# A four-layer attention and FFN kernel: the masked keys of the 16-head attentions made by VectorE, the norm's epsilon added there, a group's norm issued behind the keys ahead of it, and the mask loaded earlier

## The chip, the cores and the metric

The kernel runs on one core of a Trainium2 chip. Its time is the device time of one launch in microseconds, and the number that is compared is the median over several launches. A core has five engines with an instruction stream each: TensorE (PE in the profile; PEld is its weight load), VectorE (DVE), ScalarE (ACT), GpSimd (POOL) and SyncE (SP). An engine runs its stream in order and waits for the others by semaphores.

## The reference

`x` and `ctx_1024` are 16 blocks of 128 rows by 128 features, `mask` marks keys. Eight residual steps follow, each on the layer-normed x. This change is about the attentions of layers 0, 1 and 3:

```python
x = x + _L0_xattn_ref(_layernorm(x), ctx_1024, mask, wq, bq, wk, bk, wv, bv, wo, bo)
x = x + _L0_ffn_ref(_layernorm(x), ...)
x = x + _L1_xattn_ref(_layernorm(x), ctx_1024, ctx_1024, ...)
x = x + _L1_ffn_ref(_layernorm(x), ...)
x = x + _L2_xattn_ref(_layernorm(x), ctx_1024, ...)
x = x + _L2_ffn_ref(_layernorm(x), ...)
x = x + _L3_xattn_ref(_layernorm(x), ctx_1024, ctx_1024, ...)
x = x + _L3_ffn_ref(_layernorm(x), ...)

# layer 0's attention: 16 heads of 8 features, queries from x, keys and values from the context
attn = jnp.einsum('bhsd,bhtd->bhst', q, k) / math.sqrt(HD)
m = mask[:, None, None, :].astype(attn.dtype)
attn = attn * m - 100000.0 * (1.0 - m)
attn = jax.nn.softmax(attn, axis=-1)
o = jnp.einsum('bhst,bhtd->bhsd', attn, v)
return o.transpose(0, 2, 1, 3).reshape(b, s, NH * HD) @ wo + bo
```

Layer 1's attention scales each row of scores by a temperature that a small network reads from the scores' statistics; layer 3's is causal. The norm is `(x - m) / sqrt(v + 1e-5)`.

## The kernel before

X lies in SBUF throughout, as 16 blocks of 128 x 128 in 4 groups (NG = 4) of 4 blocks (GB = 4). Seven phases follow one another: attention of layer 0, its FFN, attention of layer 1, FFN of layer 1 together with the attention of layer 2, FFN of layer 2 (a product-key lookup), attention of layer 3, its FFN. `heads_attention` (L286) is called for layers 0, 1 and 3.

**Scores of 16 heads at once.** A head has 8 features. The 32 partitions of a row group hold 4 heads; so that one matmul with 32 rows gives the scores of 4 heads side by side, the keys K (128 x 512 of a group) are written four times into Kb, each time multiplied by a column of `c.gmask`, which keeps every fourth head and makes the rest zero (L341, L342). `s` = Q times Kb (in `negated_maxima`) gives a block's scores in two PSUM tiles of two banks, VectorE takes the negated maxima of each (L410, `nm`), GpSimd splits them into bfloat16 parts (`split`, L424 to L430), TensorE transposes them (`turn`), and the scores are computed once more, transposed and shifted (`st`), for the exponentials pT (L482, L552, L554). `av` is the sum over keys of V and of ones, `inv` (L474) the reciprocal, oT the normalized result, `po` the output projection that is added to X. In layer 1 (`warm`) GpSimd also squares the exponentials (L484).

**The order.** The loop at the end of `heads_attention` goes over steps i, in each of which different blocks are at different stages: maxima are `ahead` steps ahead of the exponentials (5, in layer 1 11). A new group's stages come with its first blocks: `begin_norm(n)`, then a step later `begin_turn(n)`, then `begin_queries(n)`. The matmuls of s, st and av are chained by `mmo`, so TensorE keeps their order; the rest of each engine's stream is put in order by the scheduler of the framework, over the whole program and by its own priorities.

**begin_norm** (L321 to L343): `layernorm` takes bn_stats and bn_aggr on VectorE (L239, L240), the reciprocal root by `rsqrt` on GpSimd, an addition of epsilon (`ve`, L231) and a power (`rstd`, L232), and then four tensor_scalars on VectorE for xn (L249, one buffer). GpSimd adds the output bias to X (L325). TensorE makes pk, VectorE (layer 0, with bias and mask, L333) or ScalarE (L337, L339) makes K of it, and GpSimd the four parts of Kb (one buffer, so that the next group's Kb waits for the last s of this one). `rsqrt` is used by all norms of the program (44 times), `begin_norm` by the three attentions with 4 groups each.

**The start.** On ScalarE's DMA queue stand the four loads of X and then the mask, broadcast to 128 partitions (L216); `mk`, a small second view of the mask, follows in layer 0's attention (L619). `pen` (L614) and `keys_out` (L621) are made of them by VectorE. The V buffers are cleared by GpSimd (L310), in space that the context's load leaves free when TensorE has transposed it.

**PSUM.** One pool of 2 one-bank buffers ("m": pt, pk, pq, pv, pm, av, po) and one of 3 two-bank buffers ("s": s and st).

Of the kernel before, what the change touches and what calls it, by code (L numbers as in the profile page):

```python
# [2 lines left out]

# [1 line left out]

# [7 lines left out]
U8 = mybir.dt.uint8  # L13
# [6 lines left out]
P = 128  # L20
NB = 16
# [159 lines left out]
def build(ctx: ExitStack, tc: tile.TileContext, x, ctxt, mask, packs, cols, out):  # L181
    nc = tc.nc
    PS = bass.MemoryType.PSUM
    const = ctx.enter_context(tc.tile_pool(name="const", bufs=1))
# [6 lines left out]
    X = const.tile([P, NB, P], F32, name="X")  # L191
    sb = {}
    widest = max(packs[name].shape[1] for name in packs)

    def load(name):

        n = packs[name].shape[1]
        if name == "c":
            t = const.tile([P, n], F32, name="consts")
        else:  # L200
            t = weights.tile([P, widest], F32, name="weights")
        nc.sync.dma_start(t[:, :n], packs[name])
        for key, (n, c, w) in cols[name].items():
            sb[f"{name}.{key}"] = t[:n, c : c + w]

    load("c")
    for n in range(NG):
        gb = slice(n * GB, (n + 1) * GB)
        nc.scalar.dma_start(X[:, gb, :], x.rearrange("b s d -> s b d")[:, gb, :])
    ident = sb["c.ident"]  # L210
    identb = const.tile([P, P], BF16, name="identb")
    nc.vector.tensor_copy(identb, ident)
    minus_half = const.tile([P, GB], F32, name="minus_half")
    nc.gpsimd.memset(minus_half, -0.5)
    mask_sb = const.tile([P, NB * P], U8, name="mask_sb")
    nc.scalar.dma_start(mask_sb, mask.rearrange("b s -> (b s)").partition_broadcast(P))  # L216

    def ps1(name):
        return psm.tile([P, 512], F32, tag="m", name=name)
# [4 lines left out]
    def mm(o, lhsT, rhs, start=True, stop=True):  # L224
        return nc.tensor.matmul(o, lhsT=lhsT, rhs=rhs, start=start, stop=stop)  # L225

    def rsqrt(o, v, eps):

        w = v.shape[-1]
        ve = small.tile([P, w], F32, tag="rs_v")  # L230
        nc.gpsimd.tensor_scalar_add(ve, v, eps)  # L231
        nc.gpsimd.tensor_tensor(o, ve, minus_half[:, :w], ALU.pow)  # L232

    def moments(xin, eps=1e-5):

        st = small.tile([P, GB, 6], F32, tag="ln_st")
        mv = small.tile([P, GB, 2], F32, tag="ln_mv")
        for b in range(GB):
            nc.vector.bn_stats(st[:, b, :], xin[:, b, :])  # L239
            nc.vector.bn_aggr(mv[:, b, :], st[:, b, :])  # L240
        rstd = small.tile([P, GB], F32, tag="ln_rstd")
        rsqrt(rstd, mv[:, :, 1], eps)
        return mv, rstd

    def layernorm(o, xin):

        mv, rstd = moments(xin)
        for b in range(GB):
            nc.vector.tensor_scalar(  # L249
                o[:, b, :], xin[:, b, :], mv[:, b, 0:1], rstd[:, b : b + 1], ALU.subtract, ALU.mult  # L250
            )
# [16 lines left out]
    def grp(n):  # L268
        return slice(n * GB, (n + 1) * GB), slice(n * GT, (n + 1) * GT)
# [16 lines left out]
    def heads_attention(pk, scale, keep=None, cmask=None, cmaskT=None, warm=False):  # L286
# [15 lines left out]
        with tc.tile_pool(name=f"at_{pk}", bufs=2) as wk:  # L302
# [5 lines left out]
            for j in range(2):  # L308
                v = wk.tile([P, GB, 4, 160], F32, name=f"V{j}", bufs=1)
                nc.gpsimd.memset(v.rearrange("p b r x -> p (b r x)"), 0.0)  # L310
                Vs.append(v)
            group = {}
# [8 lines left out]
            def begin_norm(n):  # L321
                gb, _ = grp(n)
                xn = wk.tile([P, GB, P], F32, name="xn", bufs=1)
                layernorm(xn, X[:, gb, :])
                nc.gpsimd.tensor_add(  # L325
                    X[:, gb, :], X[:, gb, :], w["bo"].unsqueeze(1).to_broadcast([P, GB, P])
                )
                group[n] = {"xn": xn, "nm": wk.tile([P, GB, 16], F32, name="nm", bufs=alive)}
                pk = ps1("pk")
                mm(pk, w["wk"], ctxT[:, grp(n)[1]])  # L330
                K = wk.tile([P, GT], F32, name="K", bufs=alive)
                if keep is not None:
                    nc.vector.scalar_tensor_tensor(  # L333
                        K, pk, w["kb"], mask_sb[:, grp(n)[1]], ALU.add, ALU.mult
                    )
                elif "kb" in w:
                    nc.scalar.activation(K, pk, AF.Identity, bias=w["kb"])  # L337
                else:
                    nc.scalar.copy(K, pk)  # L339
                Kb = wk.tile([P, 4, GT], F32, name="Kb", bufs=1)  # L340
                for g in range(4):  # L341
                    nc.gpsimd.tensor_scalar_mul(Kb[:, g, :], K, sb["c.gmask"][:, g : g + 1])  # L342
                group[n].update({"K": K, "Kb": Kb})  # L343

            def begin_turn(n):
                xT = wk.tile([P, GT], F32, name="xT", bufs=1)
# [238 lines left out]
            for i in range(-ahead - 3, NB + 2):  # L585
                pTs = exponents(i) if 0 <= i < NB else None
                if late is not None:
                    weighted(i - 1, late)
                late = pTs
                if due(i - 1 - GB) is not None:  # L590
                    finish(due(i - 1 - GB))
                if warm:
                    if squares is not None:
                        measured(i + before - 1, *squares)
                    squares = squared(i + before) if 0 <= i + before < NB else None
                if 0 <= i + ahead < NB:
                    negated_maxima(i + ahead)

                if due(i + ahead - GB) is not None:
                    turn(due(i + ahead - GB))  # L600
                if warm and due(i + 1) is not None:
                    turn(due(i + 1))
                if due(i + 2) is not None:
                    begin_values(due(i + 2))
                for k, stage in enumerate((begin_queries, begin_turn, begin_norm)):
                    if due(i + ahead + 1 + k) is not None:
                        stage(due(i + ahead + 1 + k))
# [631 lines left out]
    def layer2_ffn():  # L1239
# [6 lines left out]
        with tc.tile_pool(name="f2w", bufs=2) as wk:  # L1246
# [13 lines left out]
            def begin(n):  # L1260
                gb, _ = grp(n)
                xn = wk.tile([P, GB, P], F32, name="xn", bufs=1)
                layernorm(xn, X[:, gb, :])
                sq = wk.tile([P, GB, P], F32, name="sq", bufs=1)
                ms = small.tile([P, GB], F32, tag="ms")
                nc.vector.tensor_mul(sq, xn, xn)
                nc.vector.tensor_reduce(ms, sq, AX.X, ALU.add)
                nc.vector.tensor_scalar_mul(ms, ms, 1.0 / P)
                inv = small.tile([P, GB], F32, tag="inv")
                rsqrt(inv, ms, 1e-6)  # L1270
                nc.vector.tensor_mul(xn, xn, inv.unsqueeze(2).to_broadcast([P, GB, P]))
                xT = wk.tile([P, GT], F32, name="xT")
                transposed(xT, xn, lambda o, i: nc.vector.tensor_scalar_mul(o, i, w["norm_w"]))
                G = wk.tile([P, 8, GT], F32, name="G")
                for c in range(8):
                    pg = ps1("pg")
                    mm(pg, w["down"][:, c * P : (c + 1) * P], xT)
                    nc.scalar.activation(G[:, c, :], pg, AF.Gelu)
                group[n] = xT, G
# [203 lines left out]
```

## Time and profile before

| | us |
|---|---|
| median of 3 runs | 1607.78 (1598.61 to 1611.15) |
| the profiled execution | 1602.65 |
| its span, first to last instruction | 1600.8 |
| busy: TensorE, its weight loads | 1249.8, 880.1 |
| busy: VectorE, GpSimd, ScalarE | 957.3, 589.2, 525.4 |
| mean granted TensorE clock | 0.856 of full |
| layer 0's attention, first score matmul | 35.55 |
| layer 1's attention, first score matmul | 555.45 |
| layer 3's attention, first score matmul | 1430.10 |

The span and the busy times are of the one profiled execution; the median is of other launches, and lies 5.1 us above that execution. The profile's page gives the span in 40 slices of 40 us each. Busy shares in tenths, the granted TensorE clock in tenths, and the DMA's:

```profile
PE   4788799898989677887777756557778787878996
DVE  4566364565455665644634465557789887875552
ACT  1343455554544335554223421212001010014431
POOL 5532000000000366552222032148878878844310
PEclk7798799999999778989668977669798998889996
```

Layer 0's attention lies in the first four to five slices, layer 1's from slice 14 on (GpSimd at 3 to 6 by the squares), layer 2's lookup in slices 28 to 36 (GpSimd mostly at 7 or 8), layer 3's attention in 36 to 39. In layer 0's FFN (slices 5 to 13) GpSimd is nearly idle. An entry of the list of waits names who waited for whom, the total, how often and the longest; an entry of the timeline gives the start, the length, the engine, the line, the operation and tiles, and in brackets the idle time before and who ended it.

### The profile page before, as it was taken

The numbers are of one execution on the slowest core, as the hardware profiler recorded it, in microseconds if no ns is written. First come the engines' busy times: TensorE is split into PE (matmuls) and PEld (weight loads), VectorE is DVE, ScalarE is ACT, GpSimd is POOL, SyncE is SP. The second block draws the span as 40 slices with busy tenths as digits, with TensorE's granted clock in tenths as the row PEclk, the third lists the DMA queues.
The fourth block names the chain that finished last, engine by engine and source line by source line (L and its number), as shares of the span: only waits on it lengthen the run. The fifth ranks groups of instructions, "written<-read, shape, count | busy, mean of one in ns | idle before, by whom it ended". The sixth has DMA issues, their size and how long they took to land. (4 is left out here: it accounts for less than half of the span.)

```text
span 1600.8 us, 24944 instructions
## 1 busy us (share of the span) xinstructions
PE 1249.8 (78%) x10088; PEld 880.1 (55%) x10088; DVE 957.3 (60%) x2404; ACT 525.4 (33%) x836; POOL 589.2 (37%) x656
## 2 busy tenths in 40 slices
PE   4788799898989677887777756557778787878996
PEld 2355477676768434555555634434666666644556
DVE  4566364565455665644634465557789887875552
ACT  1343455554544335554223421212001010014431
POOL 5532000000000366552222032148878878844310
PEclk7798799999999778989668977669798998889996
DMA  4000000000000200000322020000000000000000
GB/s 150 1 2 17 0 0 1 1 0 1 1 1 1 99 1 1 2 2 2 106 68 78 24 87 1 1 9 1 1 1 1 1 1 1 1 6 1 2 2 27
DMA packets 26002, 28.05 MB, mean 18 GB/s; under 512 B 3360, under 2 KB 23712, under 8 KB 25376
## 3 DMA queue, kind: packets, MB, share of 16 engines
q1 hardware_dynamic: 20544, 23.06, 4.4%
q0 software_dynamic: 1024, 2.10, 0.4%
q10 hardware_dynamic: 4320, 1.31, 0.4%
q8 instruction: 79, 1.29, 0.3%
q14 instruction: 35, 0.29, 0.1%
HBM read 18.86 MB, written 7.60 MB: 17 GB/s over the span
## 5 line engine op out<-in xcount | busy, mean ns | idle before, releaser
L1328 POOL TENSOR_TENSOR C<-sim 128x1024 f32<-128x1024 f32 x128 | 241.5, 1919 | 48.9 <-PE psim L225 26.2
L231 POOL TENSOR_SCALAR ve<-mv 128x4 f32<-128x4 f32 x44 | 10.5, 240 | 543.6 <-DVE mv L240 516.2
L1349 PE MATMUL pc<-consts,C 128*128 128x128 f32 x1024 | 147.2, 297 | 51.3 <-POOL C L1328 26.6
L1349 PEld LDWEIGHTS pc<-consts,C 128*128 128x128 f32 x1024 | 127.2, 154 | 74.8 <-issue 38.8
L225 PE MATMUL pc<-hm,weights 128*128 128x256 f32 x640 | 155.1, 380 | 0.7 <-DVE hm L757 0.7
L1347 DVE MATCH_REPLACE8 C<-m,C 128x1024 f32<-128x1024 f32 x128 | 153.6, 1203 | 0.0
L410 DVE TENSOR_REDUCE nm<-s 128x8 f32<-128x1024 f32 x96 | 113.2, 1217 | 56.9 <-PE s L225 56.4
L225 PEld LDWEIGHTS pc<-hm,weights 128*128 128x128 f32 x640 | 120.9, 190 | 19.4 <-DVE hm L757 3.3
L474 DVE RECIPROCAL inv<-av 128x128 f32<-128x128 f32 x48 | 46.0, 957 | 109.1 <-PE av L225 109.0
L225 PE MATMUL s<-Kb,Q 32*128 32x512 f32 x384 | 76.9, 739 | 30.1 <-POOL Kb L342 25.4
L554 ACT ACTIVATE pT<-st 128x1024 f32<-128x1024 f32 x64 | 62.2, 1020 | 59.1 <-PE st L225 59.1
L225 PE MATMUL st<-Qb,K 32*128 32x512 f32 x512 | 79.4, 628 | 0.0
L342 POOL TENSOR_SCALAR Kb<-K,consts 128x512 f32<-128x512 f32 x48 | 74.4, 1567 | 9.1 <-PE s L225 9.0
L484 POOL TENSOR_TENSOR E<-pT 128x1024 f32<-128x1024 f32 x32 | 60.0, 1893 | 47.9 <-ACT pT L482 47.9
L757 DVE TENSOR_TENSOR hm<-he,M 128x512 f32<-128x512 f32 x64 | 40.7, 686 | 38.7 <-ACT he L753 38.7
L225 PEld LDWEIGHTS av<-pT,V 128*32 128x32 f32 x1536 | 42.2, 115 | 37.6 <-issue 25.8
L249 DVE TENSOR_SCALAR xn<-X,mv,rstd 128x128 f32<-128x128 f32 x112 | 51.8, 581 | 9.9 <-PE pt L257 8.2
L424 POOL CAST nms<-nm 128x16 bf16<-128x16 f32 x64 | 14.7, 255 | 116.3 <-DVE nm L410 92.6
L225 PE MATMUL av<-pT,V 128*32 128x128 f32 x1536 | 56.4, 288 | 0.6 <-DVE V L383 0.4
L225 PEld LDWEIGHTS s<-Kb,Q 32*128 32x128 f32 x384 | 23.0, 209 | 54.8 <-POOL Kb L342 30.3
L225 PE MATMUL av<-pT,consts 128*32 128x128 f32 x1536 | 52.2, 276 | 0.0
L1288 ACT COPY sim<-psim 128x512 f32<-128x512 f32 x16 | 9.4, 585 | 128.4 <-PE psim L225 128.4
(345 smaller groups left out, 2757.1 us busy)
## 6 DMA issues: line engine op xcount, KB each, us to landing
weights<-in_f SPq DMA_DIRECT2D x1, 3852.5 KB, 11.7
weights<-in_f SPq DMA_DIRECT2D x1, 2863.5 KB, 14.0
weights<-in_f SPq DMA_DIRECT2D x1, 2816.5 KB, 9.3
rows<-zero SPq DMA_DIRECT2D x2, 1344.0 KB, 11.5
rows_sb<-rows SPq DMA_DIRECT2D x14, 192.0 KB, 3.9
outs<-y SPq DMA_DIRECT2D x14, 192.0 KB, 2.0
weights<-in_a SPq DMA_DIRECT2D x1, 1088.5 KB
X<-in_x ACTq DMA_DIRECT2D x4, 256.0 KB, 5.0
```

The source lines that it names most:

```text
L225: return nc.tensor.matmul(o, lhsT=lhsT, rhs=rhs, start=start, stop=stop)
L249: nc.vector.tensor_scalar(o[:, b, :], xin[:, b, :], mv[:, b, 0:1], rstd[:, b : b + 1], ALU.subtract, ALU.mult)
L342: nc.gpsimd.tensor_scalar_mul(Kb[:, g, :], K, sb["c.gmask"][:, g : g + 1])
L410: nc.vector.tensor_reduce(nm[:, b, 8 * u : 8 * u + 8], ss[u].rearrange("p r (g k) -> p (r g) k", g=4), AX.X, ALU.max, negate=True,)
L424: nc.gpsimd.tensor_copy(at[:, b, :, :, 0], of[:, b])
L474: nc.vector.reciprocal(y, s)
L484: nc.gpsimd.tensor_mul(E2, E, E)
L554: nc.scalar.activation(pT, st, AF.Exp)
L757: nc.vector.tensor_mul(hm[:, k, c : c + 2, :], he, M[:, k, c : c + 2, :])
L1328: nc.gpsimd.tensor_add(C, sim[:, h, 0, :].unsqueeze(2).to_broadcast(sh), sim[:, h, 1, :].unsqueeze(1).to_broadcast(sh),)
L1347: nc.vector.match_replace(at, m8[:, h, :], at, 0.0)
L1349: nc.tensor.matmul(pc[:, k // 4, k % 4 * P : (k % 4 + 1) * P], lhsT=C[:, 4 * k : 4 * k + 4, :].rearrange("p i j -> p (i j)"), rhs=ident, s ...
```

## The change

```diff
     load("c")
+    mask_sb = const.tile([P, NB * P], U8, name="mask_sb")
     for n in range(NG):
         gb = slice(n * GB, (n + 1) * GB)
         nc.scalar.dma_start(X[:, gb, :], x.rearrange("b s d -> s b d")[:, gb, :])
+        if n == 0:
+            nc.scalar.dma_start(mask_sb, mask.rearrange("b s -> (b s)").partition_broadcast(P))
...
-    mask_sb = const.tile([P, NB * P], U8, name="mask_sb")
-    nc.scalar.dma_start(mask_sb, mask.rearrange("b s -> (b s)").partition_broadcast(P))
...
         ve = small.tile([P, w], F32, tag="rs_v")
-        nc.gpsimd.tensor_scalar_add(ve, v, eps)
+        nc.vector.tensor_scalar_add(ve, v, eps)
         nc.gpsimd.tensor_tensor(o, ve, minus_half[:, :w], ALU.pow)
...
                 xn = wk.tile([P, GB, P], F32, name="xn", bufs=1)
-                layernorm(xn, X[:, gb, :])
+                with tc.issue_after(group[n - 1]["last"].ins) if n else nullcontext():
+                    layernorm(xn, X[:, gb, :])
...
                 for g in range(4):
-                    nc.gpsimd.tensor_scalar_mul(Kb[:, g, :], K, sb["c.gmask"][:, g : g + 1])
-                group[n].update({"K": K, "Kb": Kb})
+                    last = nc.vector.tensor_scalar_mul(Kb[:, g, :], K, sb["c.gmask"][:, g : g + 1])
+                group[n].update({"K": K, "Kb": Kb, "last": last})
```

Four parts: the mask's load stands second in ScalarE's DMA queue, behind the first group of X; the addition of epsilon in every norm goes from GpSimd to VectorE (44 instructions); the four multiplies of Kb go from GpSimd to VectorE (48 instructions); and in the three attentions the norm of group n from 1 on is issued behind the last multiply of the group before. `tc.issue_after` puts the instructions inside behind the named one in the stream of the engine that both share, here VectorE; it adds no wait on a semaphore.

The order of the streams is made for the whole program, so the change also moves its neighbours. In the built program:

- VectorE: Kb of group 0 stands behind xn of group 0 and K (in layer 0 also behind `pen` and `keys_out`). Kb of each later group n stands between the two maxima of the last block of group n - 1 (four multiplies), and behind the second maximum come V's copy, the stats of group n + 1, `ve` and xn of group n + 1.
- GpSimd: of a norm the power alone is left. In layer 1, at group 2 the stream is power, X add, then two squares; at group 3 it is power, square, X add, square. In layer 0 the first power follows the memsets of V.
- The stats and powers of later groups of layers 1 and 3, of which some stood in the streams of the FFN ahead of them, stand in the attention itself.
- TensorE: the transposes of xn of group 1 stand ahead of s of block 3 instead of block 0; in layer 0 three of the four groups of `pv` stand behind s of block 3 instead of ahead of block 0.
- SyncE's stream is the same.

More of the change, by code (lines that the diff above doesn't have):

```diff
@@ L1 @@
 import math
-from contextlib import ExitStack
+from contextlib import ExitStack, nullcontext
 import numpy as np
```

## The prediction

> **What bounds the kernel now.** I read the busy shares first (TensorE 78%, VectorE 60%, GpSimd 37% of the span), because they say that no engine is full; then the groups of lines 225 and 342; then the list of waits, where the second entry of TensorE belongs to this change; then the timeline of each place where that wait falls; last the windows, for the clock. The chain of waits reaches back only to about 1276 us (PE 9%, DVE 5%, POOL 4% of the span), so for the attentions I go by TensorE's own waits: there it is the bound, and an idle time of TensorE ends as time.
>
> Groups (busy us, mean ns, then idle before) and list of waits (total us, times, longest):
>
> ```profile
> L225 PE MATMUL s<-Kb,Q 32*128 32x512 f32 x384 | 76.9, 739 | 30.1 <-POOL Kb L342 25.4
> L342 POOL TENSOR_SCALAR Kb<-K,consts 128x512 f32<-128x512 f32 x48 | 74.4, 1567 | 9.1 <-PE s L225 9.0
> PE s L225 <- POOL Kb L342: 25.4, 8, 4.5
> ```
>
> A quartet of key multiplies on GpSimd is 4 x 1567 ns = 6.27 us, there are 12, and 8 of them are waited for. Layer 0's attention on the timeline (start, length):
>
> ```profile
> 20.47 1.34 DVE L614 TENSOR_SCALAR pen<-mask_sb,weights 128x2048 bf16<-128x2048 uint8 x1 [1.58 <-DMA mask_sb<-in_mask]
> ...
> 23.61 4.56 POOL L310 MEMSET V<- 128x2560 f32 x2
> ...
> 29.24 6.26 POOL L342 TENSOR_SCALAR Kb<-K,consts 128x512 f32<-128x512 f32 x4
> ...
> 35.55 2.09 PE L225 MATMUL s<-Kb,Q 32*128 32x512 f32 x8 [3.95 <-POOL Kb L342]
> ...
> 48.19 6.18 POOL L342 TENSOR_SCALAR Kb<-K,consts 128x512 f32<-128x512 f32 x4
> ...
> 54.42 2.09 PE L225 MATMUL s<-Kb,Q 32*128 32x512 f32 x8 [3.36 <-POOL Kb L342]
> ```
>
> The first scores stand at the end of a row: mask lands, `pen`, norms, memset of V, an add to X, Kb, s. The keys K of group 0 were ready at 23.59 (22.85 + 0.74) and then lay 5.65 us behind GpSimd's queue. Layer 3's attention, the same row, with VectorE beside a memset:
>
> ```profile
> 1416.47 4.68 POOL L310 MEMSET V<- 128x2560 f32 x2 [18.15 <-PE po L225]
> 1416.50 2.48 DVE L1402 CAST m_causal<-consts 128x512 bf16<-128x512 f32 x1
> ...
> 1418.90 2.52 DVE L1402 CAST m_causalT<-consts 128x512 bf16<-128x512 f32 x1
> ...
> 1441.71 6.20 POOL L342 TENSOR_SCALAR Kb<-K,consts 128x512 f32<-128x512 f32 x4
> ...
> 1447.96 2.09 PE L225 MATMUL s<-Kb,Q 32*128 32x512 f32 x8 [4.08 <-POOL Kb L342]
> ```
>
> The two casts end exactly where the memset ends: VectorE is held, not merely slowed.
>
> **What the Trainium skill says.** "VectorE: DVE Perf Modes", section "The perf-mode tier table", gives a fp32 tensor_scalar in SBUF the double rate. The trace agrees: VectorE's `lo`, a tensor_scalar of the very shape of Kb, takes
>
> ```profile
> L568 DVE TENSOR_SCALAR lo<-oT x4: 426/426/428, 678.4 to 772.8; 128x512 f32<-128x512 f32 x4
> ```
>
> "GPSIMD Engine Reference", section "8. Key points", says that GpSimd shares its SBUF interfaces with VectorE's instructions in a 2-port mode or with two SBUF inputs; "Trainium Architecture — The Big Picture", section "What this means for kernel authors", calls it an exclusive lock. The casts above agree. "TensorE: Matmul & The Clock Gate", section "Part 1", says that idle windows halve the clock. Here it is 0.50 from 36 to 48 us though TensorE is busy 9.31 of 12, so I don't count on an earlier warm clock.
>
> **The change, part by part.**
>
> *Kb to VectorE.* 48 multiplies leave GpSimd (74.4 us). On VectorE one is 426 ns; queued ones follow at about 0.35 (xn, 335 ns alone, follows at 1.13 / 4 = 0.28), so a quartet is about 1.5 us. What it gives is the eight waits and what GpSimd had queued ahead of them.
>
> Layer 0: the mask's DMA goes ahead of three X loads on ScalarE's queue. Before, it landed 17.3 us after its issue at 2.99; now I put it at about 10, the X groups 1 to 3 later by the little it takes. `pen` (1.34) must then wait for the context transposes (14.1, it takes their space), as must the V memsets, which now run 14.15 to 18.7 and hold `pen` and xn. The rstd powers (4.49 for four) now stand behind the memsets for the first group. keys_out, which stands on VectorE ahead of Kb, waits for mk (issued at 14.34, 7.3 us to land: 21.6). So Kb runs at about 22 to 23.7, no later than the queries: pq and pk take TensorE until about 26.0, and s(0) starts there, between 24.3 (Q alone) and 29 (mask or mk late), instead of 35.55. That is 9.55. From there to s(4) it took 18.87, with 3.36 of wait; 1.5 of this comes back, because the new quartet stands ahead of the last maximum, and that one frees a score buffer: 1.86. **-11.4 us**, s(4) at about 43.0.
>
> Layer 1: s(0) was 1.68 behind Kb, s(4) 4.48 (Kb began at 566.24, after VectorE's maxima and the splits; the new one runs between the last two maxima). Together 6.16; about 1.2 comes back for the last maximum, as above: **-5.0** at s(4). The waits of s(8) (3.91) and s(12) (1.80) go as well: **-5.7**.
>
> Layer 3: s(0) stood at 1430.10; the query Q is ready at 1426.70 and the next pk holds TensorE till about 1427.1, so 3.0 there. At s(4) 4.08 less 0.4, since Q comes at 1443.66 and the maxima were nearly done (1443.47): 3.7. **-6.7** at s(4).
>
> *ve to VectorE (44).* 240 ns on GpSimd, one hop fewer in front of the power. Where GpSimd was queued (layers 0 and 2's FFNs), I give **-4.0** for it together with the norms that leave those phases: of groups 1 and 2 of layers 1 and 3, 4 stats and aggregates (0.28 + 0.18 each) and a 1.04 us power apiece, which stood in VectorE's and GpSimd's queues there. Bounds: 0, if they stood in idle time (VectorE 60% busy), to -6. In layer 2's attention the norm's power started right after ve; nothing to gain.
>
> *The norm behind the keys.* No semaphore, but an order on VectorE: at the turn to group n it now has Kb (1.5), stats of the next group (4 x 0.46 = 1.8), ve (0.1, an estimate from keys_out's 0.18), a wait for the power (1.1) and xn (1.1) in one row, 5.6 us; behind them are queued the next maxima (1217 each), for which TensorE's score buffers wait, and the reciprocal (957), for which the outputs wait. It was spread before. Two such turns per attention and one with Kb alone (1.5): 12.7 us per attention, 38.1 in three. Cover is VectorE's slack: 18.67 busy of 30 us in 70 to 100. In layers 0 and 3 each step has 1 to 3 us of it, so I take 0.1 + 2.4 + 0.7 and 1.6 + 2.0 + 0.6, **+7.4**; ends 0 and 25.4. In layer 1 the squares E (1893 ns each) occupy GpSimd; its queue now has the next norm's power and X add (1.1) ahead of the first squares at one turn (+2.1) and around them at the other, where xn waits behind a square under lock (1535 ns) and the squares wait for the add: +6.7, and 0.3 for the last Kb: **+9.1**; ends 2 and 21.8 (its own 12.7 on top).
>
> *Other moves.* Three pv go behind s(3), pt(1) behind s(2): TensorE's work is the same, 0. SP's queue keeps its order, ScalarE's queue has the one DMA moved; issue costs about the same, 0.
>
> Sum: -11.4 - 5.0 - 5.7 - 6.7 - 4.0 = -32.8; +7.4 + 9.1 = +16.5; **net -16.3**. The profiled execution took 1602.65 (span 1600.8), so 1586.4 of it; the median of the runs, 1607.78, is 5.1 above it: **1591.5**.
>
> **Rivals.**
>
> (a) *More gain:* the bursts lie in VectorE's slack and the clock warms earlier in layer 0 (s took 2.09 there, 1.03 to 1.14 when warm; 16 us of phase at half rate). Without the 7.4 it is -23.7, and a quarter to half of those 16 us at the warm clock gives 4 to 8: to -32. With smaller mixes -22 to -34: 1574 to 1586. For it: no wait at groups 2 and 3 of layers 0 and 3 before, so VectorE had room. Against: the clock at 36 to 48.
>
> (b) *The first step comes no earlier:* memsets, powers and mk keep Kb in layer 0 until 29, as before. Its 9.55 goes: net -6.8; -3 to -10, 1598 to 1605. This is also the case of a change that does not do what it says: the mask was only one of four things on that path.
>
> (c) *Slower:* the turns of VectorE decide. If all 38.1 us are on the path, with layer 1's 9.1 and about 4.5 more where E's or the add's lock stretches the row there, it is +51.7 against -32.8: +18.9, 1627. It is a loss once more than 32.8 - 9.1 = 23.7 of the 38.1 is exposed. For it: reciprocals and maxima are waited for by TensorE already (`st` and `s` on nm: 10.2 and 6.5 us). Against: VectorE has 40% idle.
>
> (d) *Nothing hidden is found:* GpSimd freed of 74 us moves nothing outside of the eight waits (25.4), and half of the turns (19.0) and layer 1's 9.1 eat them: +2.7; -3 to +6, 1605 to 1614.
>
> **How the numbers follow.** Main case (-10 to -22) 0.54, (a) 0.20, (b) 0.11, (d) 0.07, (c) 0.08. The forecast is the main case's 1591.5. The range 1573 to 1606 takes in the main case, nearly all of (a) and (b). About 1%, 16 us, can be told from no change: faster is half of the main case and (a), 0.27 + 0.20 = 0.47; slower is most of (c), 0.06; the rest, 0.47, is within.
>
> **What would show it.** Right: no wait of s for Kb, Kb some 430 ns each on VectorE, s(0) at 25 to 27 and s(4) at 42 to 44 in layer 0, s(4) some 5 and 7 us nearer to the start of layers 1 and 3; at the turns, new waits of TensorE on VectorE's maxima and reciprocals of 1 to 3 us each. Wrong: s(0) after 29; memsets holding Kb (then it shows 2 us or more each); turn waits above 4 us in all three attentions; or layer 1 longer than before.

## The result and the profile after

| | before | changed |
|---|---|---|
| median of 20 runs each, us | 1609.08 (1598.61 to 1614.63) | 1600.17 (1594.19 to 1605.0) |
| ratio, 95% interval | | 0.9951 (0.9936 to 0.9965) |
| profiled execution, us | 1602.65 | 1601.61 |
| its span, us | 1600.8 | 1599.8 |

The change gains 0.5%: by the ratio 7.9 us of 1609 (the two medians lie 8.9 apart). I had forecast 16.3: the right sign, inside the range, but twice the size. The two profiled executions differ by 1.0 us only, so they can't be subtracted as they stand. Cut into phases, they and a second profile of each kernel (two of the runs below) say where the time went:

| stretch (first named instruction to the next) | before, two profiles | changed, two profiles |
|---|---|---|
| start to layer 0's FFN (its first `hm`) | 176.5, 177.2 | 168.6, 171.5 |
| layer 0's FFN | 367.1, 367.5 | 367.0, 367.1 |
| layer 1's attention (`qb_s` to the first `HT`) | 243.3, 243.3 | 246.8, 246.8 |
| layer 1's FFN, layer 2's attention (to VectorE's first `C`) | 311.6, 316.1 | 315.1, 311.8 |
| layer 2's lookup (to `m_causal`) | 318.0, 313.5 | 320.4, 317.7 |
| layer 3's attention (to the first `tg`) | 147.2, 147.3 | 144.8, 144.4 |

Layer 1's and layer 3's attentions repeat to within 0.5 us and layer 0's to 3. The two phases between them scatter by 3 to 5 us each. In the kernel before, one gains what the other loses: their sum is 629.6 and 629.5. In the changed kernel it is 635.5 and 629.5. Of all seventeen profiles, those of the runs below included, twelve have 629.5 to 630.1, three 634 to 636 and two 625 to 627, and no part of the change sorts them. So the first profile of the changed kernel is some 6 us long in phases where the second is as before, and the attentions carry the result: about -7 in layer 0, **+3.5 in layer 1**, -2.7 in layer 3.

The groups of the changed kernel that answer to those of before (busy us, mean ns, idle before):

```profile
L226 PE MATMUL s<-Kb,Q 32*128 32x512 f32 x384 | 77.1, 696 | 6.8 <-DVE nm L412 2.8
L344 DVE TENSOR_SCALAR Kb<-K,consts 128x512 f32<-128x512 f32 x48 | 26.2, 607 | 0.4 <-PE s L226 0.4
```

Its list of waits (total us, times, longest):

```profile
PE st L226 <- DVE nm L412: 14.7, 15, 2.0
...
PE sm L226 <- POOL E L486: 9.9, 6, 3.2
...
PE s L226 <- DVE nm L412: 7.4, 8, 1.9
```

The wait of s for Kb, 25.4 us before, is gone, and idle time before s fell from 30.1 to 6.8. New is TensorE's wait for GpSimd's squares E, 9.9 us where it was 3.3. The start of layer 0 on the timeline:

```profile
16.29 3.33 DVE L616 TENSOR_SCALAR pen<-mask_sb,weights 128x2048 bf16<-128x2048 uint8 x1 [9.12 <-PE pt L258]
16.31 5.48 POOL L311 MEMSET V<- 128x2560 f32 x2 [7.98 <-PE pt L258]
...
19.60 2.84 DVE L250 TENSOR_SCALAR xn<-X,mv,rstd 128x128 f32<-128x128 f32 x4
...
23.69 0.17 DVE L623 TENSOR_SCALAR keys_out<-mk 128x16 f32<-128x16 uint8 x1 [0.59 <-DMA mk<-in_mask]
23.77 1.67 DVE L344 TENSOR_SCALAR Kb<-K,consts 128x512 f32<-128x512 f32 x4
...
25.23 2.08 PE L226 MATMUL pq<-xT,weights 128*128 128x512 f32 x2 [0.68 <-ACT xT L259]
27.10 1.91 PE L226 MATMUL pk<-ctxT,weights 128*128 128x512 f32 x2
28.94 1.69 PE L226 MATMUL s<-Kb,Q 32*128 32x512 f32 x8
```

A quartet of Kb is 1.67 us. The memsets hold `pen` (3.33 instead of 1.34) and xn (2.84 instead of 1.1), and s(0), the scores of block 0, starts at 28.94, 6.6 us earlier than before. Kb was ready at 25.44; what s(0) follows now is the queries' own row, pq and pk on TensorE. Next, layer 1's turn to group 3, in which the gain of that layer is lost (counted from `qb_s`, 5.4 us ahead of the kernel before at s(8), 1.2 behind it at s(9)):

```profile
594.32 1.02 POOL L233 TENSOR_TENSOR rstd<-ve,minus_half 128x4 f32<-128x4 f32 x1 [2.17 <-DVE ve L232]
595.31 1.89 POOL L486 TENSOR_TENSOR E<-pT 128x1024 f32<-128x1024 f32 x1
595.37 2.68 DVE L250 TENSOR_SCALAR xn<-X,mv,rstd 128x128 f32<-128x128 f32 x4 [1.13 <-POOL rstd L233]
...
598.13 1.09 POOL L327 TENSOR_TENSOR X<-X,weights 128x512 f32<-128x512 f32 x1 [0.93 <-DVE xn L250]
599.17 1.89 POOL L486 TENSOR_TENSOR E<-pT 128x1024 f32<-128x1024 f32 x1
601.12 1.92 PE L226 MATMUL sm<-E,consts 128*32 128x128 f32 x28 [3.23 <-POOL E L486]
```

Power, square, X add, square stand in one row on GpSimd; xn, held by the first square, stands in between on VectorE; TensorE waits at the end of it. From s(8) to s(9) it is 15.27 us, before 8.68. Not all of this is waiting. The two stretches as windows, changed kernel first (length; busy us and instructions of TensorE, its weight load, VectorE, ScalarE, GpSimd; then the granted clock, the DMA share, GB/s):

```profile
590.99:606.26 15.27, 9.38 (x93) 4.64 (x93) 10.37 (x27) 2.77 (x4) 6.75 (x8) 0.69 0.00 1
```
```profile
604.42:613.10 8.68, 7.17 (x93) 3.92 (x93) 4.57 (x8) 1.67 (x3) 4.56 (x6) 0.80 0.01 2
```

Of the 6.6 us, 4.4 are idle time of TensorE and 2.2 are the same 93 instructions at a lower clock.

### The profile page after: what moved, and what is told of

The parts are those of the page before. It is cut to its first block, busy times and chain, and to the rows that moved or that the text cites. A ratio compares the mean times of both kernels' runs of the same rounds, so it can differ in the third digit from the quotient of the medians.

```text
span 1599.8 us, 24970 instructions
## 1 busy us (share of the span) xinstructions
PE 1256.7 (79%) x10088; PEld 884.4 (55%) x10088; DVE 985.0 (62%) x2500; ACT 526.1 (33%) x836; POOL 506.0 (32%) x560
## 5 line engine op out<-in xcount | busy, mean ns | idle before, releaser
L233 POOL TENSOR_TENSOR rstd<-ve,minus_half 128x4 f32<-128x4 f32 x44 | 47.6, 1081 | 380.5 <-DVE ve L232 380.5
L311 POOL MEMSET V<- 128x2560 f32 x6 | 14.6, 2460 | 282.3 <-PE pb L855 256.4
L226 PE MATMUL st<-Qb,K 32*128 32x512 f32 x512 | 83.9, 651 | 0.0
L259 ACT COPY xT<-pt 128x512 f32<-128x512 f32 x32 | 18.8, 586 | 123.5 <-PE pt L258 123.3
```

Of the source, the lines that this page charges most:

```text
L259: (copy or nc.scalar.copy)(o, pt)
```

## The experiments

Fifteen runs; the ratios are against the kernel before on the same chip. "Kb", "epsilon", "mask" and "order" are the four parts of the change.

| run | parts in it | ratio, 95% interval | start to FFN | layer 1 | layer 3 |
|---|---|---|---|---|---|
| x_mask | mask | 1.0033 (1.0011 to 1.0055) | 182.1 | 243.3 | 149.3 |
| x_ve | epsilon | 0.9946 (0.9919 to 0.9973) | 171.4 | 243.4 | 149.9 |
| x_kb | Kb | 0.9861 (0.9821 to 0.9901) | 174.2 | 236.3 | 139.6 |
| z_kbve | Kb, epsilon | 0.983 (0.9804 to 0.9855) | 175.9 | 236.4 | 140.3 |
| x_noorder | Kb, epsilon, mask | 0.9884 (0.9843 to 0.9925) | 169.6 | 236.4 | 140.3 |
| y_order0 | as that, order in layer 0 only | 0.9847 (0.9813 to 0.9881) | 168.6 | 238.7 | 140.3 |
| y_xnonly | all, but of the order only xn's | 0.9888 (0.9849 to 0.9927) | 171.4 | 243.0 | 140.8 |
| the change | all four | 0.9951 (0.9936 to 0.9965) | 168.6 | 246.8 | 144.8 |
| y_nove | all without epsilon | 1.0 (0.9981 to 1.002) | 172.4 | 250.3 | 144.8 |

The lengths are us of the profiled execution.

**One part alone.** x_mask:

```diff
+    mask_sb = const.tile([P, NB * P], U8, name="mask_sb")
     for n in range(NG):
...
         nc.scalar.dma_start(X[:, gb, :], ...)
+        if n == 0:
+            nc.scalar.dma_start(mask_sb, ...)
...
-    mask_sb = const.tile([P, NB * P], U8, name="mask_sb")
-    nc.scalar.dma_start(mask_sb, ...)
```

> The kernel before with the mask's load alone moved to second place on ScalarE's queue. Theory (the mask is one of several things on the first row, and its 256 KB go ahead of the context's load): the context lands about 2 us later than before (12.5 instead of 10.5), pen starts earlier, but s(0) still stands behind four powers, the V memsets, an X add and Kb on GpSimd: s(0) at 33 to 37 us, ratio 0.998 to 1.002. Rival (the mask's landing was the bound): s(0) at 30 or earlier, ratio 0.996 or below.

It is 0.3% slower, a little more than I expected, with s(0) at 40.84 instead of 35.55. On VectorE's timeline:

```profile
13.30 0.29 DVE L240 BATCH_NORM_STATS2 st<-X 128x6 f32<-128x128 f32 x1 [6.39 <-DMA X<-in_x]
...
21.56 0.29 DVE L240 BATCH_NORM_STATS2 st<-X 128x6 f32<-128x128 f32 x1 [7.11 <-DMA X<-in_x]
...
23.89 1.38 DVE L615 TENSOR_SCALAR pen<-mask_sb,weights 128x2048 bf16<-128x2048 uint8 x1
```

The bound was not the mask: it now lands at 7.4, and the later X groups land later (the stats of the last two start at 21.56 and 22.63, before at 10.72 and 17.61). They stand ahead of `pen` in VectorE's stream. The order in layer 0 is what takes them from there; for s(0) the two parts are a pair.

x_ve and x_kb:

```diff
-        nc.gpsimd.tensor_scalar_add(ve, v, eps)
+        nc.vector.tensor_scalar_add(ve, v, eps)
```
```diff
-                    nc.gpsimd.tensor_scalar_mul(Kb[:, g, :], K, sb["c.gmask"][:, g : g + 1])
+                    nc.vector.tensor_scalar_mul(Kb[:, g, :], K, sb["c.gmask"][:, g : g + 1])
```

> The kernel before with the addition of epsilon alone on VectorE. Theory (it stood in slack): ratio 0.999 to 1.001, the FFN of layer 0 366 to 368 us and the lookup phase 322 to 327 us long. Rival (my prediction's -4.0 us for the queues of these phases): ratio 0.9975, both phases 1.5 to 2.5 us shorter than before.

> The kernel before with Kb's multiplies alone on VectorE; the norms keep their own places, the mask lands late. Theory (the gain is Kb's, and the norms behind the keys cost layer 1's attention some 8 us): no wait of s for Kb above 1.5 us, layer 0's s(0) at 29 to 32, and layer 1's attention shorter than before, from its first pk to layer 1's FFN 3 to 8 us less; ratio 0.990 to 0.994, so at least as good as the whole change. Rival (Kb's 1.5 us per turn is what costs in VectorE's stream): layer 1's attention as long as in the changed kernel, ratio 0.996 to 1.000.

Both gained more than any theory said. The epsilon brings 5 us in layer 0 and nothing in the phases where I had put it. Of the 5 us only 1.4 are there at s(0), and 4.4 at s(4): from 35 to 45 us the granted clock was 1.00, before 0.50. Kb alone brings 1.4%, nearly three times the whole change; layer 1 is 6.9 us shorter, and the rival of x_kb falls. Two details missed: s(0) of layer 0 came at 32.59, not by 32, and four waits for Kb, 6.2 us in all, were left, the longest of them 2.33. It stands behind the first quartet:

```profile
25.68 4.40 POOL L310 MEMSET V<- 128x2560 f32 x2
...
26.18 6.26 DVE L342 TENSOR_SCALAR Kb<-K,consts 128x512 f32<-128x512 f32 x4
...
32.59 2.09 PE L225 MATMUL s<-Kb,Q 32*128 32x512 f32 x8 [2.33 <-DVE Kb L342]
```

Beside the memsets and an X add of GpSimd behind them the quartet takes 6.26 us on VectorE, as long as it took on GpSimd.

z_kbve has both edits above.

> Kb's multiplies and the epsilon on VectorE; no order, the mask in its old place. Theory (without the order the two edits add up where the first powers run ahead): from the start to layer 0's FFN 169 to 172 us against 174.2 with Kb alone, the rest as with Kb alone; ratio 0.982 to 0.986. Rival (the epsilon's gain needs Kb on GpSimd behind it): 174, ratio 0.986 to 0.989.

The ratio came as expected, not the place: 175.9 us to the FFN in this profile (whose execution, 1588.57, was the longest of five).

**The order.** x_noorder takes it out of the changed kernel, y_order0 keeps it in layer 0:

```diff
-                with tc.issue_after(group[n - 1]["last"].ins) if n else nullcontext():
-                    layernorm(xn, X[:, gb, :])
+                layernorm(xn, X[:, gb, :])
```
```diff
-                with tc.issue_after(group[n - 1]["last"].ins) if n else nullcontext():
+                with tc.issue_after(group[n - 1]["last"].ins) if n and keep is not None else nullcontext():
```

> The changed kernel without the order of the norms behind the keys. Theory (that order puts the third power, xn and the X add between layer 1's squares; it costs about 8 us there): layer 1's attention 6 to 9 us shorter than in the changed kernel, s(8) to s(9) about 9 instead of 15.3 us; layer 0's s(0) 0 to 2 us later, since all norms stand ahead of it again; ratio 0.988 to 0.992. Rival (layer 1's loss is Kb under the squares' lock and TensorE's clock): layer 1's attention within 2 us of the changed kernel's, ratio 0.994 to 0.997.

> The changed kernel, with the order of the norms behind the keys kept in layer 0's attention only. Theory (the order pays at the start of layer 0, where it keeps the stats of late X groups out of pen's way, and costs some 10 us in layer 1 and 5 in layer 3): from the start to layer 0's FFN 168 to 170 us, layer 1's attention (its first qb_s to layer 1's FFN) 235 to 238 instead of 246.8, layer 3's (first causal cast to layer 3's FFN) 139 to 141 instead of 144.8; ratio 0.981 to 0.986. Rival (the layers' losses are Kb's place in VectorE's stream and chance): layers 1 and 3 as in the changed kernel, 0.994 to 0.996.

The order costs 10.3 us in layer 1 and 4.5 in layer 3 (x_noorder against the changed kernel), in layer 1 a little more than the theory said, and s(8) to s(9) is 8.84 again. GpSimd's squares in x_noorder, at the same block:

```profile
589.53 3.79 POOL L485 TENSOR_TENSOR E<-pT 128x1024 f32<-128x1024 f32 x2
...
592.84 1.60 PE L226 MATMUL sm<-E,consts 128*32 128x128 f32 x32
```

Two squares back to back, nothing between. At the start x_noorder's s(0) came at 35.09, 6 us later and not 0 to 2: with the mask in front and no order, all X groups' stats are ahead of `pen`. y_order0 has s(0) at 27.78 and 0.9847; its layer 1, 238.7, is a little longer than expected. Of the 7.3 us at s(0) only 0.9 are left at the FFN: from 35 to 55 us the granted clock was 0.87 in y_order0 and 1.00 in x_noorder. The ratios of the two, and that of z_kbve, which has neither mask nor order (0.983), overlap. So no run shows a gain in time from the mask and the order.

y_xnonly leaves stats, epsilon and power where they stood and orders the xn alone:

```diff
-                with tc.issue_after(group[n - 1]["last"].ins) if n else nullcontext():
-                    layernorm(xn, X[:, gb, :])
+                mv, rstd = moments(X[:, gb, :])
+                with tc.issue_after(group[n - 1]["last"].ins) if n else nullcontext():
+                    for b in range(GB):
+                        nc.vector.tensor_scalar(xn[:, b, :], ...)
```

> The changed kernel with the stats, the epsilon and the power of a group left where they stood, and the four xn multiplies alone issued behind the keys, in all three attentions. Theory (in layer 1's third turn the square of s(9)'s block waits from 592.1 to 595.3 for the power, and the rest is xn under the square's lock and the X add between squares): about half of the loss stays, layer 1's attention 240 to 244 us, s(8) to s(9) about 12 instead of 15.3. Rival A (the X add between the squares is all of it): 246 to 248. Rival B (stats and power are all of it): 235 to 239. In layer 0 the stats of all groups stand ahead of pen again: 0 to 2 us longer.

s(8) to s(9) is 12.90 us, layer 1 243.0, both as expected. But the reason that I had given for the rest is not what stands there:

```profile
593.59 1.09 POOL L332 TENSOR_TENSOR X<-X,weights 128x512 f32<-128x512 f32 x1 [1.77 <-DVE t_sq L519]
594.64 3.74 POOL L491 TENSOR_TENSOR E<-pT 128x1024 f32<-128x1024 f32 x2
```
```profile
590.68:603.58 12.90, 9.37 (x93) 4.63 (x93) 7.39 (x18) 2.77 (x4) 5.71 (x7) 0.70 0.00 1
```

The xn ran from 591.91 to 593.51, before any square, and the X add stands ahead of both squares, not between them. Of the 6.6 us at this turn, 2.4 are gone with stats and power out of the row. Of the 4.2 that stay, 2.0 are idle time of TensorE and 2.2 its work at the lower clock. In layer 3 the stats and the power are nearly all of it (140.8).

y_nove puts the epsilon back on GpSimd in the changed kernel:

> The changed kernel with the epsilon's addition back on GpSimd. Theory (alone it gained 8 us by letting the first two powers run ahead of the last X group's stats; with one norm ahead of pen there is nothing to let ahead): within 2 us of the changed kernel, ratio 0.994 to 0.997. Rival (its gain is additive): 6 to 9 us slower than the changed kernel, ratio 0.999 to 1.001.

The rival holds: without it the change gains nothing. Where the epsilon helps is less plain. s(0) of layer 0 is at 28.93, the same as with it. TensorE's clock differs: from 50 to 60 us it was 0.66 and in the changed kernel 1.00; in layer 1 s(4) to s(8) takes 32.72 us at 0.79 instead of 30.34 at 0.89. Two more runs split the epsilon in the kernel before: w_ve_heads has it on VectorE in the 12 norms of the three attentions, w_ve_rest in the other 32.

```diff
-        nc.gpsimd.tensor_scalar_add(ve, v, eps)
+        eps_on[0].tensor_scalar_add(ve, v, eps)
...
+        eps_on[0] = nc.vector if phase in (layer0_attention, layer1_attention, layer3_attention) else nc.gpsimd
         phase()
```

> The kernel before with the epsilon on VectorE in the norms of the three 16-head attentions only (12 of 44). Theory (the epsilon's 8 us are layer 0's first powers, 5 us, and the rest layer 1's FFN with layer 2's attention, where 9 of 9 profiles with it are 311.4 to 315.1 us long and 4 of 5 without it 316 to 318.6): from the start to layer 0's FFN 170 to 173 us, ratio 0.996 to 0.998. Rival (the middle phase is chance, all is layer 0's): ratio 0.993 to 0.996.

> The kernel before with the epsilon on VectorE in all other norms (32), not in the three attentions. Theory: layer 0's attention as before (176 to 178 us), layer 1's FFN with layer 2's attention 311 to 313, ratio 0.996 to 0.998. Rival (chance): that phase anywhere from 311 to 319, ratio 0.999 to 1.001.

0.9969 (0.995 to 0.9987) and 1.0008 (0.9989 to 1.0028): the 32 norms of the FFNs, the lookup and layer 2's attention give nothing that can be measured. The middle phase was 311.6 us in w_ve_rest, as the theory had it, but 310.2 in w_ve_heads too, where its norms have the epsilon on GpSimd, and the time says no gain. The start of w_ve_heads took 173.5, half a microsecond more than expected.

**The same kernels again.** z_after2 and z_before2 are one more profile of each.

> The changed kernel once more, for a second profile. Theory (the 3.5 us by which layer 1's FFN with layer 2's attention, and the 2.2 by which the lookup, were longer than in most other profiles are chance, not the change): 311 to 313 and 317 to 319 us in this one, and layer 1's attention again 244 to 248. Rival (the order of the streams makes them longer): 314 or more, and 320 or more again.

> The kernel before once more, for a second profile. Theory (its first profile was a short one, 6.5 us under the median of its runs): the same lengths in the attentions to 1 us (176.5, 243.3, 147.2), and the difference to the first profile lies in phases that no edit touches. Rival: it lies in the attentions, and then their differences between the two kernels are chance too.

The first theory holds. The lengths of the second hold too, but of the 1.2 us between the two profiles of the kernel before 0.7 lie in layer 0's attention, not in phases that no edit touches. The lengths are in the table of the result, and layer 1's 246.8 is no chance. Their single times (1597.93 and 1603.81) are no verdict.

**A step of my sum that was missing: TensorE's clock.** From s(13) to s(15) of layer 1 it is 23.73 to 23.74 us in all six profiles with Kb on GpSimd, and 27.1 to 29.0 in ten of the eleven with Kb on VectorE. Windows of 5 us from s(13) on, of the kernel before and of the changed one:

```profile
656.02:661.02 5.00, 3.59 (x21) 1.17 (x20) 4.07 (x4) 4.94 (x5) 2.89 (x2) 1.00 0.00 0
661.02:666.02 5.00, 4.86 (x33) 2.62 (x36) 3.23 (x12) 2.53 (x5) 2.05 (x6) 0.66 0.00 0
```

```profile
647.84:652.84 5.00, 4.97 (x18) 1.35 (x17) 2.58 (x3) 4.39 (x5) 2.33 (x2) 0.51 0.00 0
652.84:657.84 5.00, 4.33 (x15) 2.63 (x13) 2.30 (x4) 2.57 (x4) 1.45 (x1) 0.50 0.00 0
657.84:662.84 5.00, 5.00 (x81) 3.17 (x83) 2.40 (x9) 1.94 (x2) 3.14 (x16) 0.63 0.01 3
```

The same work has the clock at half for 13.65 us instead of 3.41. That is 3.4 us in the changed kernel and 5.0 in x_kb, which gave back part of the 11.1 us it had gained by s(13).

This is one place of several. Over the whole attention of layer 1 TensorE has the same 2758 instructions in every profile, so its busy time (with the profile's modelled ends of the matmuls) can be compared, and what is left is idle time (us, with the granted clock):

| layer 1's attention | before | the change | x_kb | x_noorder | y_nove |
|---|---|---|---|---|---|
| TensorE idle | 53.7 | 49.4 | 46.9 | 46.0 | 49.1 |
| TensorE busy | 189.6 | 197.3 | 189.4 | 190.4 | 201.2 |
| mean granted clock | 0.84 | 0.82 | 0.86 | 0.85 | 0.81 |

In the changed kernel the waits became 4.3 us shorter; the same work took 7.8 us longer. Of the order's 10.3 us, 3.4 are waits and 6.9 are work at a lower clock; the 3.5 us by which y_nove's layer 1 is longer than the changed kernel's are all of the second kind. In layer 0 the same split gives the epsilon alone (x_ve) 1.3 us more idle time and 6.4 less busy time, so its gain there is the clock's.

What makes the clock fall is open, but it is not the order of the instructions alone: z_best and z_vsplit run the same instructions in the same order on every engine in layer 1, and s(13) to s(15) takes 23.73 us in the first and 27.12 in the second. In all seventeen profiles the changes of the granted clock lie on a grid of 3.41 us, and its position sorts them: where the nearest point of the grid lies 0.08 to 1.06 us behind the start of s(13), ten profiles, the long stretch at half clock comes; where it lies 0.06 us behind or up to 0.36 ahead, seven, it does not. No run moved s(13) for this, so it is a pattern and not a shown cause.

**The memsets.** y_vlate is y_order0 with the clearing of V issued behind group 1's X add:

```diff
-                nc.gpsimd.memset(v.rearrange("p b r x -> p (b r x)"), 0.0)
...
+                if n == 1:
+                    with tc.issue_after(add.ins):
+                        for v in Vs:
+                            nc.gpsimd.memset(v.rearrange("p b r x -> p (b r x)"), 0.0)
```

> As the run with the order in layer 0 only, and the two V memsets of each attention on GpSimd issued behind group 1's X add, no longer ahead of the first norm. Theory (the memsets hold pen, xn, the causal casts and Kb by the shared port): pen 1.4 us instead of 3.3, xn of group 0 1.1 instead of 2.8 in layer 0 and instead of 4.7 in layer 1, the two casts below 1.5 us each instead of 2.5; s(0) 2 to 3 us earlier in each attention; 5 to 9 us less in all, ratio 0.976 to 0.982. Rival (the hold is moved: group 1's xn, the splits or Kb wait for the memsets there): less than 2 us in all.

0.9809 (0.9775 to 0.9843), as expected. The start and layer 1 gain (s(0) at 25.47; layer 1 232.7), and in layer 3 the hold is only moved (141.5 instead of 140.3):

```profile
1402.28 5.26 DVE L232 TENSOR_SCALAR ve<-mv 128x4 f32<-128x4 f32 x1
...
1403.12 4.40 POOL L331 MEMSET V<- 128x2560 f32 x2
1403.12 4.42 DVE L414 TENSOR_REDUCE nm<-s 128x8 f32<-128x1024 f32 x2
```

The epsilon's addition, four elements a partition, began beside an X add of GpSimd and stood 5.26 us until the memsets behind that had ended, and two maxima behind it. So z_best clears V behind the first copy of the split in layers 1 and 3, and also moves the mask's load to SyncE's queue behind the context's and mk's load to the start (`cleared` issues both memsets behind the instruction that it is given):

```diff
+                    part = nc.gpsimd.tensor_copy(at[:, b, :, :, 0], of[:, b])
+                    if n == b == 0 and keep is None and "clear" in todo:
+                        todo.pop()
+                        cleared(part.ins)
...
+        nc.sync.dma_start(mask_sb, ...)
...
+        nc.scalar.dma_start(mk, mask.rearrange("b s -> s b"))
```

> The order in layer 0 only; the V memsets behind group 1's X add in layer 0 and behind the first split copy of block 0 in layers 1 and 3; the mask's load on SyncE's queue behind the context's, and mk's at the start. Theory (in layer 3 the memsets held the tiny epsilon addition 5.3 us and the maxima behind it; here nothing of two ports runs beside them; the context lands at 10.5 again, and keys_out waits for nothing): layer 0's s(0) at 22 to 24, to its FFN 162 to 165 us; layer 3's attention 134 to 137 instead of 141.5; layer 1's 230 to 233; ratio 0.972 to 0.977, faster than both kernels. Rival (the splits of block 0 on are late now and the hold is only moved): layer 3 at 139 to 142, ratio 0.978 to 0.982.

```profile
22.45 0.18 DVE L632 TENSOR_SCALAR keys_out<-mk 128x16 f32<-128x16 uint8 x1 [6.07 <-DMA mk<-in_mask]
...
1403.12 0.92 DVE L233 TENSOR_SCALAR ve<-mv 128x4 f32<-128x4 f32 x1
...
1403.95 2.34 DVE L421 TENSOR_REDUCE nm<-s 128x8 f32<-128x1024 f32 x2
```

Layer 3 is 135.6 us, as expected; 0.9773 (0.9751 to 0.9794), just outside. The start missed: mk, issued at 3.0, still landed only at 22.4, and keys_out now stood ahead of xn in VectorE's stream, so s(0) came at 30.01 and the FFN at 170.8, where I had 162 to 165. The last run has the late memsets and leaves mask and mk as the change has them:

> The changed kernel with the order in layer 0 only and the V memsets late (layer 0: behind group 1's X add, layers 1 and 3: behind the first split copy), the mask second on ScalarE's queue and mk where it was. Theory (the version with the mask on SyncE's queue lost at the start what it was to gain, because keys_out, moved ahead of xn, waited till 22.45 for mk): s(0) of layer 0 at 25 to 26, 166 to 168 us to the FFN; layer 1's attention 229 to 233, layer 3's 135 to 137; ratio 0.972 to 0.976. Rival (layer 0's later phases lose it again): 0.976 to 0.979.

s(0) at 25.77, 168.3 us to the FFN, layer 1 232.8, layer 3 135.6. The lengths came as expected but for the start, which is 2 us longer to the FFN than y_vlate's. Its median, 1566.53, is the lowest of all, but the kernel before ran at 1600.65 on that chip: the ratio, 0.9797 (0.9757 to 0.9836), misses what I expected and the rival's too. It and z_best, which can't be told apart, beat both kernels.

## Why the prediction was right in sign and wrong in size

Every term of my sum for the attentions was a wait of TensorE, and its work was taken at one rate. The split into idle and busy time, as above for layer 1, shows what came of it (changed kernel, two profiles, against the first of the kernel before, us):

| | forecast | TensorE idle | TensorE busy |
|---|---|---|---|
| layer 0's attention | -8.2 | -4.4, -4.7 | -3.5, -0.2 |
| layer 1's attention | -1.6 | -4.3, -4.3 | +7.8, +7.9 |
| layer 3's attention | -2.5 | -2.6, -2.7 | +0.2, -0.1 |

- **The waits: right in sum.** -12.3 forecast, -11.4 and -11.8 measured. In layers 0 and 1 my shares were wrong by some 3 us each, in opposite directions; that they cancel is luck.
- **Layer 0.** s(0) came at 28.94, not 26.0: the mask's load pushed the context from 10.5 to 12.5, which I had not priced ("the little it takes"), and the memsets held more. I called pen's wait and the memsets' hold. mk stopped Kb till 23.7, not 21.6, but Kb was still ready 3.5 us before s(0). Between the two profiles of the changed kernel layer 0 differs by 3.0 us, nearly all of it busy time, at the end: from 100 to 120 us the granted clock was 0.91 in the first and 0.79 in the second.
- **Layer 1's two terms: both too large as waits.** "-5.0" and "-5.7" for Kb: x_kb has 6.8 us less idle time there. "+9.1" for the order: the changed kernel has 3.4 us more idle time than x_noorder. That the order costs 10.3 us of time, near the 9.1, is luck, since 6.9 of them are work at a lower clock. The row that I had described is there, with 6.6 us at group 3 for 6.7 forecast, but only 4.4 of them are waits.
- **Layer 3: the net right, by the same luck.** -6.7 + 4.2 = -2.5 forecast, -2.7 measured. With Kb and epsilon alone (z_kbve) the idle time is 3.9 us less and the busy time 3.0; mask and order give back 1.3 and 3.2.
- **The clock in layer 1: the term that failed first.** It is not in the sum at all. I had refused to count on a warmer clock in layer 0 and never asked what a colder one in layer 1 would cost. TensorE's work took 7.8 us longer; from s(13) to s(15) alone 3.4 us of time went. So a gain of 4.3 became a loss of 3.5.
- **The epsilon: the term that failed second.** "-4.0" for layer 0's FFN and the lookup. The FFN is the same to 0.5 us, the 32 norms outside of the attentions measure as nothing. The epsilon's gain is real (0.9946 alone, and 1.0 without it), but it lies in the attentions. In x_ve the powers at the start come one by one instead of four in a row at 19.16, which gives 1.4 us at s(0); the rest there, and all of it in y_nove's comparison of layer 1, is busy time of TensorE, and why the clock is warmer with the epsilon on VectorE no run shows.
- **Sum:** the clock, -1.8 in layer 0 on the mean of the two profiles and +7.8 in layer 1, and the FFN and lookup, +4.0, make 10.0 where I was off by 8.4.

The direction of the rivals: (a)'s warmer clock came in layer 0, where the clock was full from 43.8 us on for 31 us and before from 58.4 on, and was lost in layer 1; (b)'s mechanism was there in part; (c) did not come, the order's own waits staying below what I had taken; (d) fell, since Kb alone brings 1.4%. Of my signs of being wrong one came: layer 1 longer than before. One reading was a little too sharp: the two casts of layer 3 end 0.3 us after the memsets, not exactly with them. As for the skill, the double rate of the tensor_scalar is confirmed (607 ns mean of the 48, holds included; 1.67 us a quartet), and the exclusive lock more sharply than I had used it: it held even four elements. The page "TensorE: Matmul & The Clock Gate", section "Part 1", has the clock fall after an idle window; in the 10 us ahead of the drop in layer 1 TensorE was busy 8.71 us, and in the 10 before that 9.67, more than in the kernel before (8.45 and 8.20), where the clock fell for 3.41 us only; and in z_best the two numbers are 8.71 and 9.67 as well. So idle windows, as far as these windows show them, don't explain this drop.

Open as well: the attentions are 4 to 8 us shorter in the profiles, by pair, and the timed gain is 7.9; no run explains the scatter of the two middle phases that stands between.

## What to carry to other kernels

When work leaves a slow engine, price every edit alone, on the chip if it can be had: here one of four parts gives 1.4%, two together 1.7% (z_kbve), and all four 0.5%, which the sum hides. An instruction order that helps at one place (late loads at the start) should be written for that place; inherited by all callers it put a norm between two squares that TensorE waits for. Split a phase into idle and busy time of the engine that bounds it: where the busy time of the same instructions moves along with the granted clock, the waits are not what changed. And where VectorE and GpSimd share a lock, look for what stands beside each long GpSimd instruction, however small it is.

## What the runs showed of the hardware that I had not expected

- A VectorE addition over 128x4 f32 in SBUF took 5.26 us beside the end of a GpSimd X add and two memsets of 128x2560 f32 (y_vlate), and 0.92 beside the X add alone, when the memsets were moved away (z_best). Maxima that read PSUM ran beside the memsets there at their usual 1.2 us each.
- Kb's quartet takes 1.67 us free, 3.85 beside GpSimd's squares (layer 1, group 2 in the changed kernel), and 6.26 beside the memsets and an X add (x_kb).
- 256 KB of mask, issued ahead of three X loads, moved the landing of the context from 10.4 to 12.4 us (11.2 to 12.7 over nine profiles) and the start of the third X group's stats from 10.72 to 21.56 (x_mask).
- A stretch of layer 1 (s(13) to s(15)) repeats to 0.01 us over seven profiles with the clock at half for 3.41 us, and is 3.4 to 5.3 us longer in ten where it is at half for 13.65 us. Two kernels with the same instruction order there fall on different sides, and the changes of the granted clock lie on a grid of 3.41 us in all seventeen.
- One kernel's phase of 312 us can be 4.5 us longer in its next execution, and the phase after it 4.5 us shorter; a pair of profiles is not a measurement of half a per cent.
